# A CIN kernel: the pair table's second half made with W1's fields stationary, the start's transfers and gathers in another order, four first chunks by halves

## The chip, the cores and the metric

The kernel runs on one core of a Trainium2 chip. A core has TensorE (PE, matrix products into PSUM), VectorE (DVE), ScalarE (ACT), GpSimd (POOL) and SyncE (SP), which run side by side and wait for each other through semaphores; ACT, SP and POOL also issue DMA transfers, which 16 DMA engines carry out. The metric is the time of one execution on the device in microseconds (us). A profiled execution shows one run in detail; its span is counted from the first to the last instruction of the kernel.

## The reference: what is computed

Input `x` has 1024 samples, F = 39 fields, E = 64 elements. Three layers with H = 64 outputs each are applied, and each layer's outputs are summed over E and combined linearly:

```python
def _cin_layer(Xk, X0, W, b):
    O = W.shape[0]
    Hk, Fdim = (Xk.shape[1], X0.shape[1])
    Wr = W.reshape(O, Hk, Fdim)
    return jnp.einsum('bhe,bfe,ohf->boe', Xk, X0, Wr) + b[None, :, None]
X0 = sparse_embedding
Xk = X0
outs = []
for W, b in ((W0, b0), (W1, b1), (W2, b2)):
    Xk = _cin_layer(Xk, X0, W, b)
    outs.append(Xk.sum(axis=-1))
return jnp.concatenate(outs, axis=-1) @ fc_w.T + fc_b
```

Since the result is one number per sample, the last layer is never formed. `V2` is the last layer's weights summed with its row of `fc_w`; the second layer and the output part of the third are folded into a table T[h, a, b] = sum over o of W1[o, h, a] V2[o, b], with the second layer's row of `fc_w` as a 40th column b. Layer 1 and T both multiply products x[a] x[b] of two fields, so one set of pair products serves both: 64 rows for layer 1 (W0) and 64 rows for T.

## The kernel before, in words

**The main loop.** The samples come in 32 blocks of 32 samples: 39 rows of `BLK` = 2048 numbers. The pairs of fields are dealt into six chunks of 128 pairs, and a seventh small one for every two blocks. Five tiles `r` of 128 rows hold fields in five orders, gathered from DRAM with index lists (`roll`, `gather_rows`, line 171); the small chunk uses `u` and `v`. Chunk c of a block is the product of two of the tiles, made by VectorE (`product`, line 211; tiles 0 and 1, then 0 and 2, 3 and 1, 3 and 2, 0 and 4, 3 and 4), and TensorE multiplies it with that chunk's weights `wa` in four quarters of 512 columns (`multiply`, line 536). A product buffer is one of four. ACT and VectorE finish each block (lines 579 to 608). The order of all instructions on each engine is the order of the program text (a manual schedule); VectorE makes the product for step `at + 4` while TensorE works on step `at`.

**The start.** Before that, the weights must be made. `both` is a table of 128 rows by 39 x 40 entries (a, b): its upper 64 rows are W0 turned, by twenty transposes of `w0s` (lines 413, 450), its lower 64 rows are T. For T, four products of `w2s` with `fc2` (line 402) and two VectorE transposes (line 419) give `v2`. Then `v2`, placed twice as a block diagonal (`[128, 2, H]`), is stationary and W1 moves, ten fields at a time (line 454); the result is copied to `part` (line 465), turned by twenty transposes (line 474) and copied into `both` (line 483). From `both`, `weight_rows` (lines 501, 503) picks each chunk's entries into `pairs`, and `weight_turn` (lines 520 to 522) turns them into `wa`. `spin` (line 279) issues products that nothing reads.

**Block 0.** The index lists are computed by VectorE (lines 310 to 381). Block 0 is loaded in two halves of 16 samples into DRAM tables `xh[0]`, `xh[1]` (line 247, both on ACT's queue; the second waits for the transfer of `w2s`, whose semaphore it reuses). POOL gathers from them: tiles 0, 1, 2 of the first half, then the load of block 1 (line 165), tiles 0, 1, 2 of the second half, tile 3 of both halves, and then tile 4 from the whole block `xd`. Before these, POOL clears `pairs` and writes the rows of ones (line 345); after the gathers of block 1 it loads the biases (lines 435 to 438), then blocks 2 and 3. POOL's transfers take eight semaphores in turn, so a transfer waits for the landing of the one eight before it. The first three chunks are multiplied and loaded by halves, the fourth whole (lines 632 to 659).

Of the kernel before, what the change touches and what calls it, by code (L numbers as in the profile page):

```python
# [61 lines left out]
FH = F * H  # L62
# [4 lines left out]
NT = 5  # L67
# [10 lines left out]
BLK = 2048  # L78
NA = 10
NQ = NA // 2  # L80
NW = 20
# [63 lines left out]
def cin_kernel(ctx: ExitStack, tc: tile.TileContext, x, w0t, b0, w1, b1, w2, b2, fc_w, fc_b, out):  # L145
# [41 lines left out]

    v2 = const.tile([128, 2, H], F32, name="v2")
    bias = const.tile([H, 2], F32, name="bias")
# [27 lines left out]
    with prep as prep:  # L217
        w2s = prep.tile([128, FH // 2], F32, name="w2s")
        w1s = prep.tile([128, FH // 2], F32, name="w1s")
        w0s = prep.tile([128, NW * H], F32, name="w0s")  # L220
        part = prep.tile([FT, 4 * NA, H], F32, name="part")
        fcrow = prep.tile([1, 3 * H], F32, name="fcrow")
# [16 lines left out]
        nc.vector.memset(fc2, 0.0)  # L239
        nc.vector.memset(v2, 0.0)  # L240
        nc.vector.memset(warm, 0.0)
# [3 lines left out]

        def load_half(k):
            nc.scalar.dma_start(
                xh[k].rearrange("f (b e) -> b f e", e=E), x[k * SB : (k + 1) * SB]
            )

        load_half(0)
        for s, n in enumerate((NW, F - NW)):
# [3 lines left out]
        for s in range(2):  # L256
            nc.scalar.dma_start(
                w1s[H * s : H * s + H], w1[:, s * FH // 2 : (s + 1) * FH // 2]
            )
        load_half(1)  # L260
        nc.gpsimd.iota(place, pattern=[[0, 1]], base=0, channel_multiplier=1)
        for i in range(NT):
            at = OFFSET[i] - 3 * K + (0 if i < NT - 1 else -F)
            for k, by in enumerate((STEP[i], BASE[i], at)):
                nc.gpsimd.memset(shifts[:, k, i : i + 1], float(by))
        nc.gpsimd.iota(apart, pattern=[[1, 128]], base=0, channel_multiplier=-1)
# [19 lines left out]

        spin(3)
        spin(1, MM // 4)


# [17 lines left out]

        row, j, f0, late, v, extra = (new() for _ in range(6))
        nc.vector.tensor_copy(row, place)  # L310
        nc.vector.tensor_scalar(parity[:, 1:2], place, 1, None, ALU.bitwise_and)
# [19 lines left out]

        nc.gpsimd.tensor_copy(mask[:, 1:2], parity[:, 1:2])
        nc.gpsimd.tensor_scalar(mask[:, 0:1], mask[:, 1:2], -1.0, 1.0, ALU.mult, ALU.add)
        for s in range(2):
            nc.gpsimd.tensor_copy(fcrow2[:, :, s], fcrow[:, 2 * H : 3 * H])
# [11 lines left out]

        one = ones[0:1, 0, 0:1]
# [4 lines left out]
        nc.tensor.matmul(  # L353
            small[:, 0:1], fcrow2.rearrange("p h s -> p (h s)"), one, start=True, stop=True
        )
        nc.vector.tensor_scalar(fc2[:, 0::32], mask, small[:, 0:1], None, ALU.mult)
        nc.vector.tensor_scalar(unit, apart, 0, None, ALU.is_equal)
        for k in range(3):
            turn_row(small[0:H, k + 1 : k + 2], k)
        for k in range(2):  # L360
            turn_row(small[H:128, k + 4 : k + 5], k)
        spin()


# [34 lines left out]
        for k in range(2):  # L399
            for u in range(2):  # L400
# [7 lines left out]
                )  # L408

        for s in range(2):  # L410
# [12 lines left out]
        column = blocks.rearrange("h k (f j) -> h (k f) j", j=32)[:, :, 0]  # L423
        for s, at in enumerate((2, 5)):
            rows = slice(H * s, H * s + H)
            nc.scalar.copy(v2[rows, s, F:FT], small[rows, at : at + 1])
        for s in range(2):
            rows = slice(H * s, H * s + H)
            nc.vector.tensor_copy(v2[rows, s, 0:20], column[0:H])
            nc.scalar.copy(v2[rows, s, 20:F], column[H:128, 1:20])  # L430

        roll_small(0)
        roll(1)
        for k, t in enumerate((b1, b2)):
            nc.gpsimd.dma_start(bias[:, k : k + 1], t.rearrange("(h o) -> h o", o=1))
        for h in (0, H):
            nc.gpsimd.dma_start(b0s[h : h + H], b0.rearrange("(h o) -> h o", o=1))
        nc.gpsimd.dma_start(fcb, fc_b.rearrange("(p o) -> p o", o=1))
        load(2, nc.gpsimd)
# [21 lines left out]

        for k, a in groups:
            slots = part[:, NA * k : NA * k + NA].rearrange("b (j t) h -> b t j h", t=2)
            for s in range(2):
                copies[k % 2](
                    slots[:, :, :, 32 * s : 32 * s + 32],
                    pt[k][H * s : H * s + FT, 0 : 32 * NA].rearrange(
                        "b (h t j) -> b t j h", t=2, h=32
                    ),
                )  # L470
        turns = pw + pt[0:2]
        for k, a in groups:
            for j in range(NQ):
                nc.tensor.transpose(
                    turns[k][:, j * FT : j * FT + FT],
                    part[:, NA * k + 2 * j : NA * k + 2 * j + 2].rearrange("b a h -> b (a h)"),
                    unit[0:FT, 0:FT],
                )
        for k, a in groups:
            for t in range(2):  # L480
                lo = max(NA * k, a + NQ * t)
                n = a + NQ * t + NQ - lo
                copies[k % 2](
                    both[H:128, lo * FT : (lo + n) * FT],
                    turns[k][H * t : H * t + H, (NQ - n) * FT : NQ * FT],
                )
# [128 lines left out]
    def last_weights(pk):  # L615

        nc.tensor.matmul(pk[0:F, 0:1], v2[0:H, 0, 0:F], bias[:, 0:1], start=True, stop=True)
# [14 lines left out]
    p = {}  # L632
    for k, (n, c) in enumerate(steps[:3]):
        p[n, c] = first[k]
# [125 lines left out]
```

## Time and profile before

| what | before |
|---|---|
| runs (device time) | 735.21, 735.71, 735.70 us; median 735.7 |
| profiled execution | 735.45 us, span 733.6 us |
| granted TensorE clock, mean | 0.997 |
| TensorE busy | 726.8 us (99%) |
| VectorE busy | 641.1 us (87%) |
| ScalarE busy | 167.1 us (23%) |
| GpSimd busy | 383.9 us (52%) |
| moved by DMA | 197.25 MB, mean 269 GB/s |
| main products, line 536 | 1536 records, 666.0 us |
| products of two tiles, line 211 | 197, 434.2 us |

Busy times are sums over the span of one execution; issuing a transfer is not counted as busy. "PEld" is TensorE's load of a stationary operand, which overlaps its products. An fp32 product appears as two records of each kind. In a line such as "1.70 <-DMA r<-xh,lists" the engine was idle for 1.70 us until a transfer into `r` from `xh` landed. A busy share is an average over the whole span; what a change at the start is worth is read from the chain of waits and the timeline of the first microseconds.

### The profile page before, as it was taken

How to read it: one execution, taken by the hardware profiler on the slowest of the kernel's cores; microseconds unless marked ns; L12 is line 12 of the kernel's file. 1: busy time of each engine (PE TensorE's matmuls, PEld its weight loads, DVE VectorE, ACT ScalarE, POOL GpSimd, SP SyncE). 2: the span in 40 equal slices, each digit the busy share in tenths (PEclk: the TensorE clock that was granted, in tenths of full speed). 3: DMA queues.
4: the chain of work that ended last, by engine and by line, in shares of the span. 5: the costliest groups of instructions: out<-in, count | busy, mean ns of one | idle time of the engine just before them, and what ended most of it. 6: DMA issues, size and time to landing. Idle time of an engine off the chain costs nothing.

```text
span 733.6 us, 6425 instructions
## 1 busy us (share of the span) xinstructions
PE 726.8 (99%) x2408; PEld 317.5 (43%) x2408; DVE 641.1 (87%) x521; ACT 167.1 (23%) x244; POOL 383.9 (52%) x256
## 2 busy tenths in 40 slices
PE   8999999999999999999999999999999999999998
PEld 5434444444444444444444444444444444444443
DVE  7998888988889888898988889888898888889885
ACT  3232121221212222121221212221122221212222
POOL 7867654547555455654547545455654447545300
PEclk9999999999999999999999999999999999999999
DMA  9999868778575796757778675896757776566700
GB/s 294 404 326 374 325 259 282 291 286 327 220 276 231 300 354 247 278 233 275 299 286 299 235 277 235 308 350 224 275 242 267 326 287 263 219 248 243 287 1 0
DMA packets 63656, 197.25 MB, mean 269 GB/s; under 512 B 37684, under 2 KB 37733, under 8 KB 43656
## 3 DMA queue, kind: packets, MB, share of 16 engines
q0 software_dynamic: 29040, 186.22, 65.4%
q1 hardware_dynamic: 32894, 8.63, 5.1%
q10 hardware_dynamic: 1690, 1.99, 1.1%
q8 instruction: 19, 0.31, 0.2%
q14 instruction: 13, 0.11, 0.0%
HBM read 196.76 MB, written 10.60 MB: 283 GB/s over the span
## 4 chain that ended last, share of the span: by engine, by line
PE 96%; DMA 3%; DVE 0%; issue 0%; ACT 0%; POOL 0%
PE po L536 90%; PE po L556 4%; PE po L567 2%; DMA r<-xh,lists 1%; DMA xh<-in_x 1%; DMA w2s<-in_w 1%; DMA xd<-xh 0%; DVE p L211 0%; POOL r L171 0%; PE tr L520 0%; DVE g L586 0%; DVE sums L608 0%; ACT z L584 0%; ACT wa L521 0%; DVE y L715 0%
## 5 line engine op out<-in xcount | busy, mean ns | idle before, releaser
L536 PE MATMUL po<-p,wa 128*128 128x512 f32 x1536 | 666.0, 594 | 1.0 <-DVE p L211 1.0
L211 DVE TENSOR_TENSOR p<-r 128x2048 f32<-128x2048 f32 (+2 forms) x197 | 434.2, 2235 | 74.6 <-PE po L536 72.9
L536 PEld LDWEIGHTS po<-p,wa 128*128 128x128 f32 x1536 | 290.4, 190 | 372.2 <-issue 352.1
L171 POOL DMA_INDIRECT r<-xd,lists x156 | 300.2, 1924 | 286.8 <-issue 275.1
L584 ACT ACTIVATE z<-po,fc0s 64x512 f32<-64x512 f32 x128 | 87.4, 683 | 382.4 <-PE po L567 219.6
L586 DVE SCALAR_TENSOR_TENSOR g<-po,b0s,z 64x512 f32<-64x512 f32 x128 | 95.9, 749 | 9.3 <-ACT z L584 5.3
L579 ACT COPY g<-r 39x1024 f32<-39x1024 f32 x64 | 66.7, 1043 | 152.0 <-DVE sums L597 124.6
L597 DVE TENSOR_REDUCE sums<-g 103x16 f32<-103x1024 f32 x62 | 75.6, 1220 | 2.1
L171 POOL DMA_INDIRECT u<-xd,lists x16 | 33.4, 2086 | 4.9 <-issue 4.6
L171 POOL DMA_INDIRECT v<-xd,lists x16 | 29.4, 1838 | 4.9 <-issue 4.9
L556 PE MATMUL po<-p,wa 32*64 32x512 f32 x512 | 31.6, 600 | 0.0
L213 DVE TENSOR_TENSOR p<-u,v 128x1024 f32<-128x1024 f32 x16 | 19.5, 1216 | 0.0
L556 PEld LDWEIGHTS po<-p,wa 32*64 32x64 f32 x512 | 9.4, 131 | 20.2 <-issue 19.4
L567 PE MATMUL po<-u,wa 32*64 32x512 f32 x256 | 17.0, 587 | 0.0
L171 POOL DMA_INDIRECT r<-xh,lists x8 | 8.0, 1003 | 2.9 <-issue 1.8
L567 PEld LDWEIGHTS po<-u,wa 32*64 32x64 f32 x256 | 5.7, 132 | 8.0 <-issue 8.0
L279 PE MATMUL idle<-const-float32-1.0 128*128 128x256 f32 (+1 forms) x16 | 6.5, 555 | 0.8 <-PEq L747 0.8
L503 DVE TENSOR_TENSOR pairs<-both 128x2 f32<-128x2 f32 (+27 forms) x59 | 6.0, 170 | 0.4 <-issue 0.3
L521 ACT COPY wa<-tr 128x128 f32<-128x128 f32 x8 | 2.1, 266 | 16.9 <-PE tr L520 16.9
L165 POOL DMA_DIRECT2D xd<-in_x x5 | 5.2, 1048 | 1.3 <-DMA r<-xd,lists 1.3
L279 PEld LDWEIGHTS idle<-const-float32-1.0 128*128 128x128 f32 x16 | 4.3, 295 | 1.4 <-issue 0.7
L520 PE MATMUL tr<-unit,pairs 128*128 128x128 f32 x8 | 2.6, 320 | 1.5 <-DVE pairs L503 1.0
(101 smaller groups left out, 58.1 us busy)
## 6 DMA issues: line engine op xcount, KB each, us to landing
xd<-in_x SPq DMA_DIRECT2D x26, 312.0 KB
r<-xd,lists POOLq DMA_INDIRECT x156, 9.0
xd<-in_x POOLq DMA_DIRECT2D x5, 312.0 KB, 6.6
w2s<-in_w ACTq DMA_DIRECT2D x1, 624.0 KB
w1s<-in_w ACTq DMA_DIRECT2D x2, 312.0 KB
xh<-in_x ACTq DMA_DIRECT2D x2, 156.0 KB
xd<-xh SPq DMA_DIRECT2D x2, 156.0 KB
u<-xd,lists POOLq DMA_INDIRECT x16, 10.6
```

The source lines that it names most:

```text
L171: nc.gpsimd.indirect_dma_start(dst, None, table, bass.IndirectOffsetOnAxis(ap=lists[:, k : k + 1], axis=0))
L211: nc.vector.tensor_tensor(p[:, cols], r[:, i, cols], r[:, k, cols], ALU.mult)
L213: nc.vector.tensor_tensor(p[:, 0:SUB], ut[n // 2 % 2], vt[n // 2 % 2], ALU.mult)
L279: nc.tensor.matmul(idle[:, 0:cols], nc.const_aps.tensor(1.0, (128, 128), F32), nc.const_aps.tensor(1.0, (128, cols), F32), start=True, sto ...
L503: nc.vector.tensor_tensor(out, diagonal(a, b, sa, sb), diagonal(b, a, sb, sa), ALU.add)
L536: nc.tensor.matmul(po[n][m], wa[:, c, side : side + 2 * H], p[:, bass.ts(m, MM)], start=n % 2 == 0 and c == 0, stop=n % 2 == 1 and c == NP ...
L556: nc.tensor.matmul(dst[half * H : half * H + H], wa[rows, NPAIR, at : at + H], p[rows, bass.ts(side, MM)], start=t >= 2, stop=t < 2 and ha ...
L567: nc.tensor.matmul(dst[half : half + H], wa[rows, NPAIR + 1, H : 2 * H], ut[n // 2 % 2][rows, bass.ts(side, MM)], start=False, stop=t < 2,)
L579: nc.scalar.copy(gt[H : H + F], rt[n % 2][0:F, 0, bass.ts(m, SUB)])
L584: nc.scalar.activation(z[one], po[n][m][other], AF.Identity, bias=fc0s[other])
L586: return lambda: nc.vector.scalar_tensor_tensor(g[n][m // 2][0:H, at], po[n][m][one], b0s[one], z[one], ALU.add, ALU.mult)
L597: nc.vector.tensor_reduce(sums[:, b_at : b_at + SB], g[n][m // 2].rearrange("p (b e) -> p b e", e=E), AX.X, ALU.add,)
```

## The change

**T.** `v2` becomes one `[H, FT]` tile. For each of the 39 fields `a`, W1's 64 x 64 slice is stationary and `v2` (40 columns) moves; even fields go to the upper 64 rows of a bank and odd ones to the lower, so that the result is already turned. `part`, its copies and its transposes go; eight copies bring the banks into `both`. `w1s` lies in 64 rows instead of 128.

**Transfers and gathers.** The first half of block 0 is loaded by SP instead of ACT. Tile 3 of each half is gathered with tiles 0 to 2. The bias loads go ahead of the gathers. The clear of `pairs` is cut to the part that the small chunk needs. The fillers, the `fc2` chain, `shifts` and the small products of `fcrow` stand elsewhere.

**Four chunks by halves.** The fourth chunk joins the first three.

```diff
-    v2 = const.tile([128, 2, H], F32, name="v2")
+    v2 = const.tile([H, FT], F32, name="v2")
...
-        w1s = prep.tile([128, FH // 2], F32, name="w1s")
+        w1s = prep.tile([H, FH], F32, name="w1s")
...
-        load_half(0)
+        load_half(0, nc.sync)
...
         for s in range(2):
-            nc.scalar.dma_start(
-                w1s[H * s : H * s + H], w1[:, s * FH // 2 : (s + 1) * FH // 2]
-            )
-        load_half(1)
+            part = slice(s * FH // 2, (s + 1) * FH // 2)
+            nc.scalar.dma_start(w1s[:, part], w1[:, part])
+        load_half(1, nc.scalar)
...
-        spin(3)
-        spin(1, MM // 4)
+        spin(2)
...
+        nc.tensor.matmul(
+            small[:, 0:1], fcrow2.rearrange("p h s -> p (h s)"), one, start=True, stop=True
+        )
...
+        nc.vector.tensor_scalar(unit, apart, 0, None, ALU.is_equal)
+        nc.vector.tensor_scalar(fc2[:, 0::32], mask, small[:, 0:1], None, ALU.mult)
...
-        nc.gpsimd.memset(pairs, 0.0)
+        nc.gpsimd.memset(pairs[:, NPAIR:, 0:SQUARE], 0.0)
...
+        for k, t in enumerate((b1, b2)):
+            nc.gpsimd.dma_start(bias[:, k : k + 1], t.rearrange("(h o) -> h o", o=1))
+        for h in (0, H):
+            nc.gpsimd.dma_start(b0s[h : h + H], b0.rearrange("(h o) -> h o", o=1))
+        nc.gpsimd.dma_start(fcb, fc_b.rearrange("(p o) -> p o", o=1))
...
-        spin()
+        spin(2)
...
         for k, cols in enumerate(halves):
-            for i in range(3):
+            for i in range(4):
                 gather_rows(rt[0][:, i, cols], xh[k], i)
             if not k:
                 load(1, nc.gpsimd)
         for k, cols in enumerate(halves):
             nc.sync.dma_start(xd[0][0:F, cols], xh[k])
-        for k, cols in enumerate(halves):
-            gather_rows(rt[0][:, 3, cols], xh[k], 3)
         roll(0, (4,))
...
-        w1v = w1s.rearrange("o (h f) -> o h f", f=F)
-        groups = [(k, min(NA * k, F - NA)) for k in range(4)]
-        for k, a in groups:
+        w1v = w1s.rearrange("o (h f) -> o f h", f=F)
+        for a in range(F):
+            q, g, t = a // (2 * NQ), a // 2 % NQ, a % 2
             nc.tensor.matmul(
-                pt[k][:, 0 : 32 * NA],
-                v2.rearrange("o s b -> o (s b)"),
-                w1v[:, :, a : a + NA],
+                pt[q][H * t : H * t + H, g * FT : g * FT + FT],
+                w1v[:, a],
+                v2,
                 start=True,
                 stop=True,
             )
...
+        for q in range(4):
+            for t in range(2):
+                a = 2 * NQ * q + t
+                m = len(range(a, min(F, 2 * NQ * (q + 1)), 2))
+                copies[t](
+                    bothv[H:128, a : a + 2 * m - 1 : 2],
+                    pt[q][H * t : H * t + H, 0 : m * FT].rearrange("h (a b) -> h a b", b=FT),
                 )
-        spin()
-        spin(1, MM // 4)
-        first = [prods.tile([128, BLK], F32, name="p", tag="p") for _ in range(3)]
+        spin(3)
+        first = [prods.tile([128, BLK], F32, name="p", tag="p") for _ in range(4)]
...
-    for k, (n, c) in enumerate(steps[:3]):
+    for k, (n, c) in enumerate(steps[:4]):
...
-    for n, c in steps[:3]:
+    for n, c in steps[:4]:
         product(n, c, halves[1], p[n, c])
-    n, c = steps[3]
-    weight_rows(c)
-    p[n, c] = product(n, c)
-    for k, (n, c) in enumerate(steps[:3]):
+    for k, (n, c) in enumerate(steps[:4]):
         multiply(n, c, p[n, c], (0,))
-        if k < 2:
+        if k < 3:
             weight_turn(steps[k + 1][1])
         multiply(n, c, p[n, c], (1,))
...
-        if at < 3:
+        if at < 4:
             quarters = quarters[2:]
-        if at < NPAIR and at > 1:
+        if at < NPAIR and at > 2:
```

More of the change, by code (lines that the diff above doesn't have):

```diff
@@ L78 @@
 BLK = 2048
-NA = 10
-NQ = NA // 2
+NQ = 5
 NW = 20
@@ L218, in cin_kernel @@
         w2s = prep.tile([128, FH // 2], F32, name="w2s")
-        w1s = prep.tile([128, FH // 2], F32, name="w1s")
+        w1s = prep.tile([H, FH], F32, name="w1s")
         w0s = prep.tile([128, NW * H], F32, name="w0s")
-        part = prep.tile([FT, 4 * NA, H], F32, name="part")
         fcrow = prep.tile([1, 3 * H], F32, name="fcrow")
@@ L239, in cin_kernel @@
         nc.vector.memset(fc2, 0.0)
-        nc.vector.memset(v2, 0.0)
         nc.vector.memset(warm, 0.0)
@@ L244, in cin_kernel, with load_half @@
         nc.scalar.dma_start(w2s, w2.rearrange("o (s n) -> (o s) n", s=2))
-        def load_half(k):
-            nc.scalar.dma_start(
+        def load_half(k, engine):
+            engine.dma_start(
                 xh[k].rearrange("f (b e) -> b f e", e=E), x[k * SB : (k + 1) * SB]
             )
-        load_half(0)
+        load_half(0, nc.sync)
         for s, n in enumerate((NW, F - NW)):
@@ L256, in cin_kernel @@
         for s in range(2):
-            nc.scalar.dma_start(
-                w1s[H * s : H * s + H], w1[:, s * FH // 2 : (s + 1) * FH // 2]
-            )
-        load_half(1)
+            part = slice(s * FH // 2, (s + 1) * FH // 2)
+            nc.scalar.dma_start(w1s[:, part], w1[:, part])
+        load_half(1, nc.scalar)
         nc.gpsimd.iota(place, pattern=[[0, 1]], base=0, channel_multiplier=1)
[L262 to L265, printed above, removed]
         nc.gpsimd.iota(apart, pattern=[[1, 128]], base=0, channel_multiplier=-1)
@@ L309, in cin_kernel @@
         row, j, f0, late, v, extra = (new() for _ in range(6))
+        nc.vector.tensor_scalar(parity[:, 1:2], place, 1, None, ALU.bitwise_and)
+        nc.gpsimd.tensor_copy(mask[:, 1:2], parity[:, 1:2])
+        nc.gpsimd.tensor_scalar(mask[:, 0:1], mask[:, 1:2], -1.0, 1.0, ALU.mult, ALU.add)
+        for i in range(NT):
+            at = OFFSET[i] - 3 * K + (0 if i < NT - 1 else -F)
+            for k, by in enumerate((STEP[i], BASE[i], at)):
+                nc.gpsimd.memset(shifts[:, k, i : i + 1], float(by))
+        for s in range(2):
+            nc.gpsimd.tensor_copy(fcrow2[:, :, s], fcrow[:, 2 * H : 3 * H])
+        one = ones[0:1, 0, 0:1]
+        nc.tensor.matmul(
+            small[:, 0:1], fcrow2.rearrange("p h s -> p (h s)"), one, start=True, stop=True
+        )
         nc.vector.tensor_copy(row, place)
-        nc.vector.tensor_scalar(parity[:, 1:2], place, 1, None, ALU.bitwise_and)
         step(row, F, 1.0, j)
@@ L330, in cin_kernel @@
         nc.vector.tensor_scalar(lists[:, NT : 2 * NT], fields_of, float(FT), None, ALU.add)
[L332 to L335, printed above, removed]
         for k, series in enumerate((U_STEPS, V_STEPS)):
@@ L345, in cin_kernel @@
             nc.gpsimd.dma_start(xd[k][F::FT].rearrange("r (p c) -> p r c", c=128), ones)
-        one = ones[0:1, 0, 0:1]
+        for k, t in enumerate((b1, b2)):
[3 more added lines that the diff above has]
+        nc.gpsimd.dma_start(fcb, fc_b.rearrange("(p o) -> p o", o=1))
         def turn_row(dst, k):
             nc.tensor.matmul(dst, fcrow[:, k * H : k * H + H], one, start=True, stop=True)
[L353 to L361, printed above, removed]
-        spin()
+        spin(2)
         r, most, seat, far = (new() for _ in range(4))
@@ L408, in cin_kernel @@
                 )
+        for k in range(3):
+            turn_row(small[0:H, k + 1 : k + 2], k)
+        turn_row(small[H:128, 4:5], 0)
         for s in range(2):
@@ L423, in cin_kernel @@
         column = blocks.rearrange("h k (f j) -> h (k f) j", j=32)[:, :, 0]
[L424 to L430, printed above, removed]
+        nc.scalar.copy(v2[:, F:FT], small[0:H, 2:3])
+        nc.vector.tensor_copy(v2[:, 0:20], column[0:H])
+        nc.scalar.copy(v2[:, 20:F], column[H:128, 1:20])
         roll_small(0)
         roll(1)
[L434 to L438, printed above, removed]
         load(2, nc.gpsimd)
@@ L460, in cin_kernel @@
             )
[L462 to L469, printed above, removed]
-                )
[L471 to L486, printed above, removed]
-        spin()
-        spin(1, MM // 4)
-        first = [prods.tile([128, BLK], F32, name="p", tag="p") for _ in range(3)]
+        for q in range(4):
[5 more added lines that the diff above has]
+                    pt[q][H * t : H * t + H, 0 : m * FT].rearrange("h (a b) -> h a b", b=FT),
+                )
+        spin(3)
+        first = [prods.tile([128, BLK], F32, name="p", tag="p") for _ in range(4)]
     def weight_rows(c):
@@ L615, in last_weights @@
     def last_weights(pk):
-        nc.tensor.matmul(pk[0:F, 0:1], v2[0:H, 0, 0:F], bias[:, 0:1], start=True, stop=True)
+        nc.tensor.matmul(pk[0:F, 0:1], v2[0:H, 0:F], bias[:, 0:1], start=True, stop=True)
         nc.tensor.matmul(pk[0:1, 1:2], bias[:, 0:1], fc[:, 1:2], start=True, stop=False)
```

## The prediction

> **What bounds the kernel now.** The page comes first: TensorE (PE) is busy 99% of the span and the chain that ended last is 96% PE. The page's list of groups gives the unit of that work: one 128x128 by 128x512 fp32 product is two records, and the chain of waits runs 96 records in 41.40 us, so 0.862 us per product. These products are the same before and after. What can move is only the time until PE has its work without a gap. So I read the chain of waits from 0 to 46 us:
>
> ```profile
> 0.74 4.18 DMA w2s<-in_w
> 4.94 6.32 DMA xh<-in_x
> 11.28 2.48 DMA xd<-xh
> 14.06 0.94 POOL r L171
> 15.30 6.85 DMA r<-xh,lists
> 22.18 1.23 DVE p L211
> 23.55 6.25 PE po L536 x14
> 29.90 1.72 PE po L536 x4
> 31.73 3.44 PE po L536 x8
> ```
>
> Up to 22.15 us the chain is transfers, then one VectorE (DVE) product, then PE; later only one hole is left (0.47 us at 39 us). The chain names the gather issued at 15.30: tile 3, first half, asked for behind the second halves of tiles 0 to 2. In the merged timeline of DVE (start, length, group, idle time before it) its price stands:
>
> ```profile
> 15.50 0.89 DVE L503 TENSOR_TENSOR pairs<-both 128x4 f32<-128x4 f32 x6 [0.28 <-issue]
> 16.30 0.68 DVE L211 TENSOR_TENSOR p<-r 128x512 f32<-128x512 f32 x1
> 19.48 0.99 DVE L503 TENSOR_TENSOR pairs<-both 128x4 f32<-128x4 f32 x10
> 22.18 4.63 DVE L211 TENSOR_TENSOR p<-r 128x1024 f32<-128x1024 f32 x4 [1.70 <-DMA r<-xh,lists]
> ```
>
> Call T the start of the first product, 16.30. It waits for the pair table `both` (complete at 15.41), not for its gathers, which landed by 13.8 (issued 7.79, 6.0 to landing). The third place is the table of windows, one row per us (busy PE, PEld, DVE, ACT, POOL; then clock, DMA share, GB/s):
>
> ```profile
> 9.00:10.00 1.00, 1.00 (x12) 0.58 (x10) 0.46 (x1) 0.00 (x0) 0.92 (x1) 1.00 1.09 246
> 10.00:11.00 1.00, 1.00 (x17) 0.87 (x16) 0.92 (x4) 0.71 (x3) 1.00 (x2) 1.00 1.09 413
> 16.00:17.00 1.00, 0.47 (x2) 0.50 (x3) 0.99 (x5) 0.00 (x0) 0.69 (x2) 0.75 1.00 410
> 19.00:20.00 1.00, 1.00 (x3) 0.55 (x2) 1.00 (x7) 0.21 (x2) 1.00 (x1) 0.54 1.04 406
> ```
>
> The DMA engines are full from 3 us on: until 10 us with the start's small-piece loads (208 to 258 GB/s from 5 us on), then with gathers at 400. And PE's clock is halved from 16.5 to 19.9 us, after its idle microsecond.
>
> **What the Trainium skill says.** "DMA: Bandwidth & Descriptors", section "Queues, rings and completion order": an engine takes its queues in turn, a packet of descriptors at a time. The trace agrees in kind: three 16 KB writes `xd<-ones` need 6.1 to 6.7 us to land while the loads run. Same page, "Anatomy of one DMA — SWDGE (gpsimd) path": about 2.0 us fixed plus bytes over 436 GB/s; for one 512 KB gather an estimate of 3.2 us. The trace never shows so little (6.0 at least), but never an early gather on free engines either. "TensorE: Matmul & The Clock Gate", Part 1 ("The HAM clock gate"): full clock is withdrawn or given after a window of 3.4 us; 16.5 to 19.9 is one such window. Same page, Part 3 ("Packing small matmuls"): products that write different column strips run at the same time; no row here isolates that.
>
> **The change, part by part.**
>
> *First four chunks by halves; tile 3's first half gathered before the second halves.* After T, before, DVE needs 0.60 (product), 0.77 (rows of chunk 1), 1.81 (three products), 0.99 (rows of chunk 2): T+4.17. Then it stood 1.70. After: chunk 2's first half (4.63/4 = 1.16) to T+5.33, chunk 3's rows (1.06, overlapping slightly) T+6.35, chunk 3's first half T+7.5, and 0.14 later PE (23.41 to 23.55 in the chain): T+7.6. From there PE has ten products to chunk 4's first: 10 x 0.862 + one transpose 0.11 gives T+16.33. Before, that product began at 31.73 + 3 x 0.862 = 34.31, T+18.01. At equal T this is worth 1.68. DVE ends chunk 4 at T+15.0, 1.3 ahead of PE (before 34.31 - 32.90 = 1.4), so DVE is no new bound.
>
> *PE's part of the start.* Line 402 needs `w2s` (landed 4.92) but began at 7.09, behind a filler (5.93 to 7.15). Now fillers come earlier: two of 0.95 (3.33 us for three and a half) to 2.7, the `fcrow2` product 0.58 to 3.4, two more fillers to 5.3. Then line 402's 2.40 to 7.7, four small products (five took 0.82) 8.4, twenty transposes 1.28 to 9.7; half clock makes it 10.5. `v2` is complete 1.06 after line 402's end, as before: 8.8. `w1s` keeps its place in ACT's queue, and only 10.63 is known as its latest landing. I take 10.0 as start of the T products (9.7 to 10.6; before 10.63).
>
> *T itself.* Removed: four products (10.63 to 13.21), eight `part` copies, twenty transposes, eight copies; they ended at 15.41. Added: 39 products, 78 records, each a load of 64 columns and 40 moving columns. Nearest rows: the twenty `pw` transposes, 1.28/20 = 64 ns per record, and the ten records of line 351, 0.82/10 = 82 ns at half clock. Lower bound 32 ns (0.82 halved is 41, and two strips may overlap): 2.5 us. Upper bound: the skill's load price (same TensorE page, "LDWEIGHTS (loading the stationary operand)": columns/1.2, 53 ns) plus 33 ns moving, nothing hidden: 87 ns, 6.8 us. I take 50 ns, 3.9 us. Then copies: ACT's copy of a bank now waits for DVE's, since their rows of `both` interleave: 0.38 + 0.33 + handovers, 1.0. Rows of chunk 0: 0.80 (15.50 to 16.30). T = 10.0 + 3.9 + 1.0 + 0.8 = 15.7, 0.6 earlier.
>
> *Gathers.* On POOL the `pairs` clear shrinks from 0.94 to about 0.1, so the three `ones` writes begin at 3.5, not 3.93. But the five bias loads now stand before the first gather: 1.17 + 1.10 + 0.63 = 2.90 us of POOL time, to 8.2. They also take semaphores: eight serve POOL's DMAs in turn, three `ones` and five biases fill them, and the first gather now waits for the first `ones` to land: 3.5 + 6.1 to 6.7, about 10.0, against 6.43. Behind it stand all gathers and load(1). The second follows 1.25 later, 11.25. Landing takes 6.0 at worst as before, 3.2 at best (skill); the loads are over by then, so I take 4.0: 15.25, inside T. The second halves: POOL reaches tile 1's at about 17.75 (four gathers of 1.25, load(1) 1.08 plus pauses), landing by 21.8 at 4.0; DVE wants it at T+7.5 = 23.2. The later gathers come 3 us later than before: tile 4 of block 0 is issued near 21.8, lands in 8.2, 30.0, wanted near 28.4 to 30.0; its margin is thin. Block 1's first two tiles land near 34 to 36; DVE wants them at 35.4 but PE only at 42.
>
> *Costed at nothing.* The index list: DVE's line 303 took 1.39 instead of about 0.2 beside POOL's `pairs` clear and is freed, but the list now waits for the `fc2` product; ready near 5.8, covered by the gathers' wait to 10.0. `xh` half 1 no longer waits for `w2s` (3.5 instead of 4.94): same cover. `xh` half 0 moves to SP behind `fcrow` and shares the engines with `w2s`: up to 0.6 on line 402 if uncovered. Half clock after T: six products must be done by T+7.6; at half until 19.9 they end 0.3 later. I charge 0.3.
>
> *Sum.* 1.68 + 0.6 - 0.3 = 2.0. The profiled execution took 735.45 (span 733.6, 1.85 around it): 733.45. The runs' median is 0.25 above it: 733.7.
>
> **The rivals.** (1) *T's products are slow* (87 ns, or half clock): T = 18.6, gain 1.68 - 2.3 = -0.6: 736.3. For it: 78 records replace 28; against: 64 ns for the transposes. (2) *DMA only trades one late tile for another*: with 6.8 us to landing, as at 14.06, tile 1's second half lands at 24.5, DVE stands 1.3: 735.0. For it: DMA full from 3 to 40 us; against: the engines drain before the first gather. (3) *Slower: the semaphore wait holds the gathers.* If the first gather starts at g and landing takes 6.0, T = g + 7.25. Gain is zero at T = 18.0, g = 10.7; past g = 12.2 the kernel is slower by over 0.2%. At g = 13 (the `ones` writes starved behind two load queues) T = 20.2: 738.0. For it: the writes already need 6.7; against: they are issued earlier and the loads' bytes are the same.
>
> **Chances.** A measurement of this kernel can tell about 0.2%, 1.47 us, from no change. Forecast 0.55, rival 1 0.15, rival 2 0.14, rival 3 0.13, the rest 0.03. The forecast's own range is T 15.0 to 16.3: 732.7 to 734.2. Rivals 1 and 2 lie within 0.2%. Range 732.5 to 736.6, which leaves out rival 3 and little else. Faster 0.57, same 0.30, slower 0.13.
>
> **What would show it.** First product at 15.7, and no DVE wait for `r` before chunk 4; first gather near 10.0; T's products 3.9 us from 10.0; chunk 4's first PE product near 32.3. The prediction is wrong if DVE's first long wait is on a gather, if PE works on T past 15 us, or if a later hole opens.

## The result and the profile after

The changed kernel takes 738.36 us (median of 14 executions, 737.32 to 741.54) against 735.65 for the kernel before (14 executions, 735.21 to 737.87): a ratio of 1.0041, with a 95% interval of 1.0028 to 1.0054. (Here and below the ratio is estimated from the single executions, so it differs a little from the quotient of the medians.) It is slower by 0.4%, where I had forecast 733.7. The profiled execution took 737.74 (span 736.0, where before had 733.6).

The whole difference arises in the first 45 us. The clearest mark is the start of block 0's join on TensorE, the small-chunk products of 32x512, in the timelines of before and after:

```profile
42.13 1.97 PE L556 MATMUL po<-p,wa 32*64 32x512 f32 x32
...
44.45 1.97 PE L522 MATMUL po<-p,wa 32*64 32x512 f32 x32
```

From there to the end both spans have 691.5 us left. I use this mark for the runs below.

GpSimd's timeline of the changed kernel (start, length, group, idle time before it and what ended it), from the writes of ones to block 0's fifth tile:

```profile
3.27 1.81 POOL L344 DMA_DIRECT2D xd<-ones  x3
5.06 1.07 POOL L348 DMA_DIRECT2D bias<-in_b  x2
7.13 0.54 POOL L351 DMA_DIRECT2D fcb<-in_fc_b  x1
11.40 1.06 POOL L170 DMA_INDIRECT r<-xh,lists  x1 [3.73 <-DVE both L435]
...
25.26 3.95 POOL L170 DMA_INDIRECT r<-xd,lists  x1 [0.30 <-issue]
```

GpSimd is done with the bias loads at 7.67 and then stands 3.73 us. The engine named as releaser, VectorE, isn't what it waited for: the first gather is the ninth DMA of GpSimd, and the program lets it wait for the semaphore of the first write of ones. By the record of semaphores in the trace that write landed at 10.58, 7.3 us after its issue, and the gather started 0.82 us later. The windows of 1 us (columns as in the prediction) show what stands idle meanwhile:

```profile
10.00:11.00 1.00, 0.86 (x13) 0.73 (x12) 0.93 (x2) 0.55 (x2) 0.00 (x0) 1.00 0.18 58
11.00:12.00 1.00, 1.00 (x22) 1.00 (x20) 0.00 (x0) 0.37 (x1) 0.60 (x1) 1.00 0.00 0
```

The loads are over and the DMA engines move nothing. VectorE's timeline, to be compared with the lines of before shown above:

```profile
16.32 0.66 DVE L469 TENSOR_TENSOR pairs<-both 128x4 f32<-128x4 f32 x6 [0.35 <-ACT both L450]
18.69 0.69 DVE L210 TENSOR_TENSOR p<-r 128x512 f32<-128x512 f32 x1 [1.71 <-DMA r<-xh,lists]
...
24.92 3.48 DVE L210 TENSOR_TENSOR p<-r 128x1024 f32<-128x1024 f32 x3
28.95 2.36 DVE L210 TENSOR_TENSOR p<-r 128x1024 f32<-128x1024 f32 x2 [0.55 <-DMA r<-xh,lists]
...
33.95 2.29 DVE L210 TENSOR_TENSOR p<-r 128x2048 f32<-128x2048 f32 x1 [1.95 <-DMA r<-xd,lists]
```

The first product starts at 18.69 instead of 16.30, because its rows were gathered late. The old stop of 1.70 us ahead of the second halves has shrunk to 0.55, so that edit did its work; but a new stop of 1.95 stands before chunk 4, which needs the fifth tile. The chain of waits, from that tile's gather on:

```profile
25.26 8.57 DMA r<-xd,lists
33.83 0.03 issue
...
33.95 2.30 DVE p L210
36.26 0.14 issue
36.39 1.10 PE po L502 x2
```

Chunk 4's first product on TensorE starts at 36.39, where before had 34.31: 2.1 us, nearly all of the 2.3 at the join. T itself is not in this chain. TensorE's timeline shows how it fared:

```profile
8.48 1.91 PE L407 MATMUL pw<-unit,w0s 39*128 39x39 f32 x20
10.53 2.69 PE L439 MATMUL pt<-v,w1s 64*64 64x40 f32 x40
12.96 2.61 PE L439 MATMUL pv<-v,w1s 64*64 64x40 f32 x38
15.50 2.93 PE L271 MATMUL idle<-const-float32-1.0 128*128 128x256 f32 x6
```

T's 78 records take 5.0 us (10.53 to 15.57), 65 ns each, where I had taken 50. All of this ran at about half clock, by the durations: a warm-up record took 488 ns (the last line), 230 in before at 14.59 us. The clock column, 1.00 in the rows of windows above, doesn't show it here. The pair table is complete at 16.3, later than before (15.41), but hidden behind the gathers.

### The profile page after: what moved, and what is told of

Its sections match the earlier page's. It is cut to its first block, busy times and chain, and to the rows that moved or that the text cites. A ratio compares the mean times of both kernels' runs of the same rounds, so it can differ in the third digit from the quotient of the medians.

```text
span 736.0 us, 6511 instructions
## 1 busy us (share of the span) xinstructions
PE 730.0 (99%) x2456; PEld 319.9 (43%) x2456; DVE 638.3 (87%) x516; ACT 164.9 (22%) x238; POOL 392.3 (53%) x256
## 4 chain that ended last, share of the span: by engine, by line
PE 95%; POOL 1%; DMA 1%; DVE 1%; issue 1%; ACT 0%; DVEq 0%; POOLq 0%
PE po L502 88%; PE po L522 4%; PE po L533 2%; POOL r L170 1%; DMA r<-xd,lists 1%; PE pv L393 0%; DVE p L210 0%; PE idle L271 0%; PE pw L407 0%; DVE both L435 0%; POOL xd L164 0%; DVE g L552 0%; PE small L354 0%; DVE sums L574 0%; ACT z L550 0%
## 5 line engine op out<-in xcount | busy, mean ns | idle before, releaser
L170 POOL DMA_INDIRECT r<-xd,lists x156 | 306.1, 1962 | 278.9 <-issue 269.5
L170 POOL DMA_INDIRECT v<-xd,lists x16 | 34.7, 2172 | 4.9 <-issue 4.9
L170 POOL DMA_INDIRECT u<-xd,lists x16 | 29.1, 1820 | 4.9 <-issue 4.9
L170 POOL DMA_INDIRECT r<-xh,lists x8 | 10.3, 1292 | 5.9 <-DVE both L435 3.7
L271 PE MATMUL idle<-const-float32-1.0 128*128 128x256 f32 x16 | 8.1, 662 | 0.8 <-PEq L710 0.8
```

The source lines that it names most:

```text
L170: nc.gpsimd.indirect_dma_start(dst, None, table, bass.IndirectOffsetOnAxis(ap=lists[:, k : k + 1], axis=0))
L271: nc.tensor.matmul(idle[:, 0:cols], nc.const_aps.tensor(1.0, (128, 128), F32), nc.const_aps.tensor(1.0, (128, cols), F32), start=True, sto ...
```

## The experiments

Two theories stood after the result. W: the bias loads fill GpSimd's eight semaphores, the gathers start late, and everything follows from there. P: T's own products, slow at half clock (the transposes take 1.91 against 1.28 before), hold the start.

**Bias loads and gathers.** In *a1* the five bias loads go back behind block 1's gathers; in *a2* they stay and the writes of ones go behind the first four gathers; *b1* does the converse, the kernel before with the bias loads ahead; *b2* gives the kernel before the new order of gathers and the fourth chunk by halves, with its old T.

```diff
 # a1; b1 does the reverse on the kernel before
-        for k, t in enumerate((b1, b2)):
-            nc.gpsimd.dma_start(bias[:, k : k + 1], t.rearrange("(h o) -> h o", o=1))
...
         load(3, nc.gpsimd)
+        for k, t in enumerate((b1, b2)):
+            nc.gpsimd.dma_start(bias[:, k : k + 1], t.rearrange("(h o) -> h o", o=1))
...
 # b2, on the kernel before
-            for i in range(3):
+            for i in range(4):
                 gather_rows(rt[0][:, i, cols], xh[k], i)
-    for k, (n, c) in enumerate(steps[:3]):
+    for k, (n, c) in enumerate(steps[:4]):
```

> The changed kernel with the five bias loads put back behind the gathers of block 1. Theory W (the gathers were held by the semaphores that the bias loads occupy): the first gather starts near 7.4, when xh's first half lands (7.1), not at 11.4; the first product then waits for the pair table, complete at 16.3, and starts at 17.0; chunk 4's first PE product near 33.4 to 33.7 against 34.3 in the kernel before and 36.4 in the changed one; 734.9 us (734.3 to 735.6). Theory P (T's products and the halved PE clock hold the start): the first product stays at 18.7 or PE stays late, 737 us or more.

> The changed kernel with the bias loads left ahead of the gathers, but the three writes of ones moved behind the four gathers of the first half, so that three gathers find free semaphores. Theory W: POOL reaches the first gather at about 6.5 and starts it near 7.4; about as with the bias loads moved back, 735.0 us (734.3 to 735.9). If it were POOL's time for the bias loads and not the wait, the first gather would come only the 1.8 us of the three writes earlier, at 9.6, and the time would be near 737. Theory P: 737 or more.

> The kernel before with only the five bias loads moved ahead of the gathers. Theory W: the first gather starts near 11.3 instead of 6.4; tile 3's first half, still ninth in POOL's order, lands 5 to 6 us later and VectorE's stall of 1.7 grows to 7: 741 us (739 to 743). If only POOL's time counts (2.6 us): 738. Theory P: no more than 736.

> The kernel before with only the gather order (tile 3 with tiles 0 to 2 of each half) and the fourth chunk by halves. The prediction's term for this was 1.68 us at an equal first product: 734.0 us (733.6 to 734.5), no VectorE wait for a gather before chunk 4. Rival (one late tile for another): a wait of 1.3 to 1.7 for a second half's tile appears and the time is 735.0 to 735.7.

Measured, against 735.52 for before on the same chip: a1 736.49 (ratio 1.0014, 1.0001 to 1.0026), a2 737.00 (1.0019, 1.0006 to 1.0031), b1 740.19 (1.0060, 1.0044 to 1.0076), b2 735.74 (1.0000, 0.9992 to 1.0008). The chain of waits of b1:

```profile
20.50 6.29 DMA r<-xh,lists
26.80 0.02 issue
26.82 1.27 DVE p L211
28.09 0.14 issue
28.23 7.76 PE po L536 x14
```

and the first gather in GpSimd's timeline of b1, then of a2:

```profile
11.61 1.06 POOL L171 DMA_INDIRECT r<-xh,lists  x1 [3.26 <-issue]
...
7.76 1.06 POOL L170 DMA_INDIRECT r<-xh,lists  x1 [1.56 <-DVE lists L372]
```

With nothing but the bias loads moved, the kernel before starts its first gather at 11.61 instead of 6.43 and its second halves 4.6 us late (26.82 for 22.18), and its median is 4.7 us up. (The profiled execution, 741.62, lost 6.2: the 4.6, and 1.5 because the 14 records shown took 7.76 us instead of 6.25.) W holds, and the part of the change that I had filed among the starts of gathers is its dearest. In a2 the first gather starts at 7.76 although the five bias loads still precede it: the semaphores are what held it, not GpSimd's 2.6 us of issuing. But neither a1 (forecast 734.9) nor a2 (735.0; theory P had its 737) is faster than before, so W is not all. And b2, forecast at 734.0, shows no gain from the new order alone: its first product starts at 18.11 and the join at 42.59. VectorE did not stop for gathered rows before chunk 4; T was late. W1 landed only 0.25 us later than in before, but T's four products (eight records) ran at about half clock:

```profile
10.88 2.19 PE L452 MATMUL pt<-w1s,v 128*128 128x320 f32 x4 [2.02 <-DMA w1s<-in_w]
12.86 2.13 PE L452 MATMUL pv<-w1s,v 128*128 128x320 f32 x4
```

These took 4.1 us where before had 2.6 (granted clock 0.50 from 12 to 13 us), so b2's profile doesn't show the new order at an equal T.

**T's pace.** *c2* is a1 with two more warm-up products ahead of the transposes, which open TensorE's clock; *b3* is the kernel before with only the new T; *e1* is a1 with each stationary operand read from 64 neighbouring columns of W1. In e1 other columns of W1 stand in for those of the field, which changes T; counts and shapes are the same.

```diff
 # c2: ahead of the small products
+        spin(2)
 # e1
-                w1v[:, a],
+                w1s[:, H * a : H * a + H],
```

> After with the bias loads back in their old place, and two more warm-up products (4 records of 256 columns) on TensorE behind the products of L393, ahead of the small products and W0's transposes. Theory P (T's products run at half clock because TensorE's work from 5 to 10 us is too thin to open its clock): the granted clock is full before T's products start, their 78 records take 2.6 to 3.4 us in place of 5.3, the first product of chunk 0 starts at 15 to 15.7 in place of 17.2. If the start then carries to the end, the time is 1 to 1.5 us below that of the kernel without the warm-up (736.5): 735.0 to 735.5. Theory U (block 1's gathers, whose issue drags beside VectorE's products, set the end of the first stage): the first product is early all the same, and the time stays at 736 to 737, with the wait of VectorE for block 1's first tile longer by what the start gained.

> The kernel before with the new computation of T alone (W1 on 64 rows, 39 products with W1's fields stationary, 8 copies, no transposes of T); transfers, gathers and the order of the chunks as before. T's new products at half clock take 5 us against 4.3 for the old ones with their copies and transposes at mostly full clock. The first product starts at 16 to 17.3 (16.3 before), but VectorE stops for gathered rows near 18 to 22 as before, which takes this up: 735.3 to 736.0, no change. If T's computation itself cost something (theory P carried to the end), it would be 736.5 to 737.

> After with the bias loads back in their old place, and T's 39 products reading their stationary 64x64 operand from 64 neighbouring columns of W1 instead of every 39th (the weights are then the wrong ones, so T is wrong; counts and shapes are the same). In the kernel with the warm-up products T's products took 66 ns per record at full clock and at half clock alike, so the clock doesn't set them. Theory L (the strided read of the stationary operand sets the pace): 35 to 50 ns per record, 2.8 to 3.9 us for 78 records in place of 5.3, weight loads below the 212 ns each seen there. Rival (a fixed cost of each weight load and 40-column product sets it): 62 to 70 ns per record as before. Time 735 to 739 in either case.

c2 took 737.11 (ratio 1.0018, 1.0010 to 1.0027) and b3 736.12 (1.0003, 0.9995 to 1.0012, before 735.64); e1, a single execution, 732.60, below its forecast of 735 to 739. TensorE's timeline of c2:

```profile
10.37 1.18 PE L403 MATMUL pw<-unit,w0s 39*128 39x39 f32 x20
11.47 2.64 PE L440 MATMUL pt<-v,w1s 64*64 64x40 f32 x40
```

and of e1:

```profile
8.32 1.19 PE L402 MATMUL pw<-unit,w0s 39*128 39x39 f32 x20
9.44 1.36 PE L439 MATMUL pt<-v,w1s 64*64 64x40 f32 x40
10.62 1.95 PE L439 MATMUL pv<-v,w1s 64*64 64x40 f32 x38
```

In c2 the transposes run at full speed (1.18 for 1.91), and T's products still take 66 ns per record, the same as in the changed kernel at half clock: theory P falls, the clock does not set them (and the first product came at 17.89, later than a1's 17.11, since the warm-ups themselves pushed the transposes back). c2's time met neither of its two forecasts; b3 is near the expected no change. In e1 the first 40 records take 34 ns each; the other 38 take 51, since the granted clock was halved from 11.1 us on. So with neighbouring numbers the clock does count, and with the stride hardly. What differs is only the stride of the stationary operand: one field of W1 is every 39th number of a row. The profile of one tile gives a load of such an operand as 212 ns in c2 and 135 ns in e1 (the first 40 records of each, mostly at full clock). The Trainium skill has the likely mechanism on "SBUF — State Buffer", section "Door 1: The DMA port swizzle (why `[64,N]` ≈ `[32,N]`)": SBUF is read in lines of 16 bytes, and an access that crosses to a new line pays, so that four fp32 numbers are as far as one strides for free. A stride of 39 is a new line for every number. The trace agrees in the direction (212 for 135); that the lines are the cause, and what other strides cost, no run here shows.

**The two causes crossed.** W1 is handed over with its 64 columns of one field side by side, as W0 already is; the instructions stay the same. *f1* is a1 with this, *f2* the changed kernel with this, *f3* the kernel before with new T and this.

```diff
-        "w1": L0_rec_W1,
+        "w1": np.asarray(L0_rec_W1).reshape(H, H, F).transpose(0, 2, 1).reshape(H, F * H),
...
-        w1v = w1s.rearrange("o (h f) -> o f h", f=F)
+        w1v = w1s.rearrange("o (f h) -> o f h", f=F)
```

> After with the bias loads back in their old place and W1 handed to the kernel with its 64 columns of one field side by side, as W0 is already, so that T's stationary operands are neighbouring columns; otherwise the same instructions. Theory L (strided read of the stationary operand): T's 78 records take 2.8 to 3.5 us in place of 5.3, the first product starts at 15.2 to 15.9 (17.2), block 0's join on TensorE at 39.3 to 40 in place of 41.6 to 42.4, and the time is 732.3 to 734, faster than before. Theory U (VectorE's run of products holds a gather, whatever T does): T is early, and the time is 735 to 737 all the same.

> The changed kernel with W1 handed over field by field and nothing else; the bias loads stay ahead of the gathers. Theory W (the start is the first gather's start plus 7.3 us, T is off the path): T is done near 14 in place of 16.3, the first product still waits for gathered rows and starts at 18.0 to 18.8, and the time is 737.3 to 738.5, that of the changed kernel. If T's pace was what cost the changed kernel its time (theory L alone), 734.5 to 736.

> The kernel before with the new computation of T and W1 handed over field by field; gathers in the old order, and the first four chunks as before. The first product starts at 14.5 to 15.5 in place of 16.3, then VectorE stops for the second halves of the gathered rows till about 22 as in before, so that the join stays at 42 to 42.8: 735.2 to 736.0. If T alone were worth anything: 733.5 to 734.5.

Measured against 735.59: f1 734.36 (732.54 to 738.58; ratio 0.9992, 0.9977 to 1.0007), f2 739.12 (1.0053, 1.0041 to 1.0066), f3 737.51 (1.0023, 1.0011 to 1.0034). VectorE's timeline of f2, in which T is done by 12.9:

```profile
12.90 0.66 DVE L469 TENSOR_TENSOR pairs<-both 128x4 f32<-128x4 f32 x6 [0.35 <-ACT both L450]
18.44 0.69 DVE L210 TENSOR_TENSOR p<-r 128x512 f32<-128x512 f32 x1 [4.88 <-DMA r<-xh,lists]
```

The first product starts at 18.44 all the same (18.69 in the changed kernel): as W says, T was off the path there, and a T 3.4 us sooner gains nothing. (f2's 739.12 lies above its forecast, 737.3 to 738.5.) Without the bias loads ahead, in f1, a faster T counts, 14.93 for a1's 17.11, though the first product again waits for rows last:

```profile
14.93 0.69 DVE L210 TENSOR_TENSOR p<-r 128x512 f32<-128x512 f32 x1 [0.78 <-DMA r<-xh,lists]
```

Its join starts at 39.99, and its profiled span is 731.5: the state that I had forecast for the change. Eight of its fourteen executions (732.5 to 734.5) lie below every execution of before on that chip (735.12 at best), but six lie at 736.0 to 738.6, and the interval includes 1; f1 is not shown to be faster. The profiled execution is one of the eight.

f3 was expected to be no different from before, and is slower. Its chain of waits:

```profile
22.26 1.26 DVE p L211
23.52 0.14 issue
23.66 7.94 PE po L511 x14
```

and the same records in TensorE's timelines, of f3 and of before:

```profile
23.66 7.94 PE L511 MATMUL po<-p,wa 128*128 128x512 f32 x14 [3.12 <-DVE p L211]
...
23.55 6.25 PE L536 MATMUL po<-p,wa 128*128 128x512 f32 x14 [0.96 <-DVE p L211]
```

VectorE resumes at the same time as in before (22.18), since the second halves are gathered as late. But T's early end left TensorE a hole of 3.12 us ahead of 23.66 (0.96 in before), and the next 14 records took 7.94 us in place of 6.25, with the granted clock at 0.50 from 24.4 to 27.9 (in before it was full there). The same 14 records took 7.94 in the run with a pause (below), behind a hole of 3.02 and again with half clock for 3.4 us. An early start behind which a longer wait opened cost TensorE its clock, here 1.7 us.

**What holds the later gathers.** In a1's profile the gather for `u` took GpSimd 6.37 us to issue, beside five half-chunk products of VectorE in a row, and block 1's tiles came late (its join at 41.56 was early, but TensorE then stood 2.2 us, behind a VectorE that had stood 6.60 for block 1's rows). This profile is of one of a1's slower executions, 738.81 in a range of 734.99 to 739.37. Its lines for VectorE and TensorE:

```profile
44.27 2.29 DVE L210 TENSOR_TENSOR p<-r 128x2048 f32<-128x2048 f32 x1 [6.60 <-DMA r<-xd,lists]
...
46.61 12.23 PE L502 MATMUL po<-p,wa 128*128 128x512 f32 x24 [2.22 <-DVE p L210]
```

*c3* puts a pause into that row, *g1* (on f1) and *g2* (on a1) break it by moving the sums of weight rows for chunks 4 and 5 into it; *d1* shortens the warm-up behind T, *d2* also moves the writes of ones to SP's queue.

```diff
 # c3
+    for _ in range(24):
+        nc.vector.tensor_copy(pause[:, 0:3], small[0:H, 1:4])
     for n, c in steps[:4]:
         product(n, c, halves[1], p[n, c])
 # g1, g2: behind the first and third of these products (and no longer later)
+        if k in (0, 2):
+            weight_rows(steps[4 + k // 2][1])
 # d1, d2
-        spin(3)
+        spin(1)
```

> After with the bias loads back in their old place, and a pause on VectorE of 24 small copies from PSUM (about 1.5 to 2 us) ahead of the second halves of the first four chunks' products. Theory U: GpSimd's issue of the gather for u (6.37 us beside VectorE's products in the kernel without the pause) ends inside the pause: 2 to 3.5 us, and block 1's gathers land 3 to 4 us sooner; TensorE's hole of 2.2 us at the start of block 1 shrinks below 1 us. The pause costs VectorE 1.5 to 2 us of a lead that block 1's wait would have taken up anyway: 735 to 736.5. Rival (the issue is long for a reason of its own, such as the number of its descriptors): the issue stays at 5 to 7 us, the hole stays, and the time is 736.5 to 738.

> After with the bias loads back in their old place, and one warm-up product behind T (2 records) in place of three (6 records, 2.93 us at half clock). In the kernel with three, the last warm-up ended at 18.65 and the first transpose of weight rows started at 18.44, though its rows were done at 17.2. Theory S (these warm-ups hold the start): first transpose about 17.3 to 17.6, first product on TensorE about 1 us sooner than 19.4, provided the clock isn't open later for it. If the start carried to the end, 735.5; theory U (GpSimd's gathers set the end of this stage, see the pause) says it is given back: 736 to 737.

> As the kernel with one warm-up product, and the writes of ones on SP's queue instead of GpSimd's, so that nothing of GpSimd's holds its eight semaphores or its time ahead of the gathers. The first gather starts at 7.1 to 7.6 (8.7 with ones on GpSimd), the gathers of u and v are issued by 19 to 23, before VectorE's run of five half-chunk products (from about 23) that held one of them for 6.4 us. Theory U: the hole of 2.2 us at block 1 is gone in most executions, and the time is 734.5 to 735.7, not above before's. Rival: another gather is held as long, with block 1's later tiles late instead: 736 to 737.5.

> The kernel with bias loads back and W1 field by field; the sums of weight rows for chunks 4 and 5 now stand between the second halves of the first four products (behind the first and the third), where they stood behind the fourth and behind chunk 4's product. VectorE's row of five half-chunk products (5.87 us) is then cut to rows of two. Theory U: no gather's issue before 32 us takes over 4 us, and the executions at 736 to 738.6 are gone: median 732.5 to 734.3, faster than before. Rival (the slow executions have another cause, such as late transfers): the same two groups, median 734 to 736.

> The same reordering with W1 as in the changed kernel (T's products at 66 ns per record) and the bias loads back. Theory U: the upper group of the kernel without the reordering (738.3 to 739.4) is gone: 734.8 to 736.0. Rival: 736 to 737 as without it.

GpSimd's timeline in a1:

```profile
23.70 6.37 POOL L170 DMA_INDIRECT u<-xd,lists  x1 [0.30 <-DVE pairs L469]
30.38 2.61 POOL L170 DMA_INDIRECT v<-xd,lists  x1 [0.30 <-issue]
```

and in c3:

```profile
24.16 1.68 POOL L170 DMA_INDIRECT u<-xd,lists  x1 [0.30 <-DVE pairs L469]
26.15 0.93 POOL L170 DMA_INDIRECT v<-xd,lists  x1 [0.30 <-issue]
```

With VectorE reading PSUM instead of multiplying two SBUF tiles, the same gather is issued in 1.68 us and the next in 0.93: the long issue comes from VectorE's products. "GPSIMD Engine Reference", section "1. Specifications", says that GpSimd shares its SBUF interfaces with VectorE, with contention under VectorE instructions that have two SBUF inputs; 6.37 against 1.68 us is its price here. As a cure c3 was useless: the pause took 4.46 us where I had taken 1.5 to 2, and the kernel 740.53 (1.0060, 1.0043 to 1.0077).

d1 took 737.43 (1.0023, 1.0011 to 1.0034, before 735.76) and d2 737.04 (1.0013, 1.0002 to 1.0023). In both another gather, the one for `v`, met the row of products and took 6.36 us, which was d2's rival expectation; d2's earlier start (first product on TensorE at 18.46, 19.40 in a1) did not reach the end: in its profile the join came at 41.48, 0.65 sooner than in before, but 692.7 us followed it instead of 691.5; VectorE stood 3.47 us for block 1's first tile. g1 took 735.20 (732.33 to 737.29; 0.9994, 0.9981 to 1.0006, before 735.51) and g2 736.00 (1.0003, 0.9992 to 1.0014). Before 30 us no issue in g1 or g2 took over 3 us, so the row is what made 6.4 us of it; in g2 the next row, 5.62 us of products from 29.90, held a gather for 6.03. But g1's executions still spread over 5 us with no gap, and its median isn't below f1's; it lies where the rival expectation had it, which had looked for two groups. g2's median is at the edge of both of its expectations. So the long issue is real, and that it explains the slower executions of f1 is not borne out. What makes them stays open: no slower execution of f1 and no faster one of a1 was profiled. One more candidate no run tests: with the bias loads in their old place they land at 43.5 us (f1) to 53 (a1), near the time at which VectorE first reads them for block 0, and in b2's profile VectorE stood 1.0 us for them.

A second profile of the kernel before, *c0*, says how much the start varies by itself.

> The kernel before once more, for a second profile of the first 25 us: how much the landing of W1 (9.6 to 10.5 us) and TensorE's clock before 17 us differ from execution to execution. 735.2 to 736.0 us.

It took 735.82. Its T products began at 11.26, behind W1's landing, where the first profile has 10.63; and its join at 42.53 for 42.13, with the gathers' stop absorbing the rest.

## Why the prediction was wrong

*Gathers: the step that failed.* The prediction's term for the gathers has the first one start near 10.0 and its rows land 4.0 us later, "inside T". I had named the semaphore wait and put its end at "about 10.0", from the landing of 6.1 to 6.7 us that the writes of ones had in before. In the changed kernel the first of them, issued at 3.27 among the starting loads, took 7.3 us, and the gather began 0.82 us after that landing, a handover that the sum doesn't have (b1: landed 10.79, begun 11.61): 11.40. Then I let the gathers land in 4.0 because the loads would be over. They were over (0 GB/s from 11 to 12 us), and for a gather with the engines to itself 4.0 is right: the first one landed after 4.0 us in b1 and 4.1 in f2. But the first product needs tiles 0 and 1, and the second gather, issued while the first was moving, took 5.8: issued at 12.76 instead of 11.25, it landed at 18.60 instead of 15.25. My estimate of 3.2 from the Trainium skill ("DMA: Bandwidth & Descriptors", section "Anatomy of one DMA — SWDGE (gpsimd) path") is short of even the lone gather, and of the one that counted by nearly half: the measurement decides. So it was the gathers, and not the pair table, that let the first product go, at 18.69 instead of 15.7.

I had forecast chunk 4's first product near 32.3 and it came at 36.39. Of these 4.1 us, nearly all of the 4.3 by which the profiled execution missed (737.74 for 733.45), 3.0 come from T and 1.1 from the fifth tile. Rival 3's own formula, T = g + 7.25, gives 18.65 for g = 11.40; measured 18.69. Its mechanism and its sign came true. Its formula alone makes that a loss of only 0.65 us, the rest being the fifth tile; so that its figure of 738.0, for g = 13, lies near the measured 738.36 is luck.

*The fifth tile: margin "thin", and gone.* T + 16.33, with the charge of 0.3, would give 35.3 for chunk 4's first product; it was 36.39. Its gather was forecast to be issued near 21.8 and to land at 30.0; it was issued at 25.26 and landed at 33.83. Of the 3.5 us of delay 1.1 had come by the second half's tile 1 (issued at 18.88 for 17.75), and 2.3 came after it, since the three issues ahead of the fifth tile's took 1.32, 2.27 and 1.87 us beside VectorE's products where I had counted 0.94 and a pause. Here late gathers fell beside VectorE's products, where each was dearer: the delay fed itself.

*T itself: inside its bounds, at the wrong value.* 65 ns per record against 50 taken (32 to 87). I had looked at the load's columns and not at their stride. In the changed kernel this cost nothing, the gathers being later still. Once they are freed it counts: first product at 17.11 in a1 and, with rows again the last to come, at 14.93 in f1.

*By halves: right in size as far as it shows, and conditional.* Equal T gives 1.68: in b2 the join comes 24.48 after the first product, in before 25.83, so 1.35 was kept. But b2's first product came 1.8 us later than before's, and before has a stop of 1.70 in which such a delay can vanish; the term pays only if T is early.

*Costed at nothing:* rightly for the index list, which showed no wait of its own. For `xh` only under the cover of the semaphore wait: its first half, now on SP's queue, landed at 7.87 in a1 (5.59 in before), and with the bias loads back it is what the first gather waits for, until 8.71. The charge of 0.3 for half clock was small beside the rest. Rivals 1 and 2 did not decide, though each named a true weakness: T's products are slow, and one late tile was traded for another, the fifth for the one ahead of the second halves.

## What to carry to other kernels

Before moving small loads ahead of a gather, count the DMAs that the queue has in flight: the one that reuses a semaphore waits for the oldest to land, and a tiny write issued among the starting loads can take as long as they do (here 7.3 us). Where the load of a stationary operand sets the pace, read it from neighbouring numbers, and lay the weights out so in DRAM. And two edits can hide each other: the new order of gathers alone gained nothing (b2) and a fast T alone lost 1.9 us (f3), while with both the profiled join came at 39.99 instead of 42.13 (f1), though a lower time is not shown. Cross them before judging either.

## What the runs showed of the hardware

- A gather of 512 KB on idle DMA engines landed 4.0 us (b1) and 4.1 us (f2) after its issue; those issued behind it while it moved took 5.6 (b1, f2) and 5.8 to 6.2 (the changed kernel).
- A 16 KB write issued at 3.27 us among the starting loads took 7.3 us to land, and the gather that waited for it began 0.82 us later.
- A 64x64 fp32 stationary load with a stride of 39 numbers took 212 ns, 135 with neighbouring ones, both mostly at full clock; product and load together 66 and 34 ns per record. At half clock they took 65 to 70 and 51.
- A gather's issue on GpSimd took 0.94 us alone, up to 6.4 beside a row of VectorE products of two SBUF tiles, and 1.68 beside VectorE's copies from PSUM.
- 14 records took 7.94 us behind a hole of 3 us on TensorE, with the granted clock at 0.50 for 3.4 us of them, and 6.25 behind a hole of 0.96, at full clock.
